# Two layers over a graph on one core: fewer completion signals from the matrix engine, and more edges counted instead of gathered

## The chip, the core and the metric

The kernel runs on one core of a Trainium2 chip. The metric is the device time of one launch in microseconds. Three runs of the kernel before took 3515.92, 3524.63 and 3525.21 us; the median is 3524.63 us.

The engines have separate instruction queues and signal each other with semaphores. PE multiplies matrices, DVE and ACT work on vectors, POOL issues indirect DMAs (it gathers rows of a table by a list of indices), and SP issues plain DMAs. "PEld" in the profile is PE's loading of the operand that stays in the array. Products land in PSUM[...].

## What is computed

There are 12500 nodes with 32 features, and 200000 edges sorted by their target `dst`. Two residual layers follow each other:

```python
h = relu(layernorm(x))
# layer 0
h  = h * rsqrt(max(out_degree, 1))[:, None]
x  = x + (segment_sum(h[src], dst) * rsqrt(max(in_degree, 1))[:, None]) @ W + b
h = relu(layernorm(x))
# layer 1, for each edge
msg = concat([h[dst], h[src] - h[dst]])
m   = relu(relu(relu(msg @ W1 + b1) @ W2 + b2) @ W3 + b3) @ W4 + b4
x   = x + segment_sum(m, dst) / max(count(dst), 1)[:, None]
```

## The kernel before

Edges are handled in tiles of 128 and chunks of four tiles (`TPC` = 4, 512 edges, 391 chunks). The order on each engine is the order in which the program is written out: the code is traced under a manual schedule, and generators (`scale_rows`, `multiply`, `count_edges`, `update_nodes`) are advanced by hand so that their stages interleave.

**Degrees.** For each batch of `HG` groups of `HT` = 4 tiles DVE makes two one-hot tiles (`hi`, `lo`, line 325) from the upper and lower part of `src`, and PE adds their products (line 342) into one table of counts. Three buffers of each exist. Meanwhile POOL gathers the raw rows of the first `EARLY` = 64 chunks (`rows_early`). After the degrees, the normalised features are split into three bf16 terms and written to the table `tab_hn`.

**Layer 0.** The chunks go three ways:
- The first 64 chunks were gathered before the degrees were known. `scale_rows` looks their scale up by one-hot products (`look`, line 664), scales the rows, and sums them by target with `sum_rows` (line 628) into `ps_early`; every fourth chunk the sum is added to an accumulator.
- Chunks 64 to `DIR` - 1 are gathered, four indirect DMAs a chunk (`gather_chunk`, line 211), and summed by `sum_rows` into `ps_late`, two steps later (`LAG`). Eight buffers `rows` lie between POOL and PE.
- The `ND` tiles from chunk `DIR` on are not gathered, but counted: for a tile, three products of one-hots (line 766) give a table of how often each of 98 x 128 sources is used by each of 13 targets, ACT copies each of the three ranges of the table out of PSUM (line 767), and `multiply` multiplies the counts of eight tiles with the whole table of features, kept in SBUF, by 98 products (line 721). The result is turned and put in its place by `L730` and `L740`.

One loop drives all this: step `m` gathers chunk `m`, prepares a one-hot for chunk `m + 2`, advances the counting by its share of `stages`, advances `scale_rows` and one stage of one `update_nodes`, and sums chunk `m - 2`. A group of 512 nodes whose sums are complete is queued for `update_nodes`, which has six stages (lines 474 to 514) and ends by writing the two tables `tab_i` and `tab_j` of the second layer. Updates run one after another.

**Layer 1.** 196 pairs of chunks pass through a pipeline. At step `m`, POOL gathers the eight tiles of pair `m` from `tab_j` (`gj`, six buffers), and PE runs the fourth product of pair `m - 5` (sum by target, line 918), the third of `m - 4` (line 900), the second of `m - 3` (line 888) and the first of `m - 1` (transposes of the gathered rows, line 870, and the products with the target rows, line 874). ACT applies the first two relus (lines 878 and 891), DVE the third (line 903).

Of the kernel before, what the change touches and what calls it, by code (L numbers as in the profile page):

```python
# [8 lines left out]
F32 = mybir.dt.float32  # L9
BF16 = mybir.dt.bfloat16  # L10
# [6 lines left out]
P = 128  # L17
# [3 lines left out]
HID = 64  # L21
# [28 lines left out]
NQ = -(-NBLK // J)  # L50


HG, HT = 2, 4
AHEAD_HG = 3


EARLY = 4 * GRP * J
# [4 lines left out]

DIR = 300
ND = NTR - DIR * TPC
TD = 8
GD = TD // TPC
# [16 lines left out]
def gnn_kernel(  # L85
# [497 lines left out]
    def halves(m):  # L583
        return [k for k in range(2) if 2 * m + k < NCH]
# [4 lines left out]
    with tc.tile_pool(name="e0", bufs=8) as sp, tc.tile_pool(name="nu", bufs=1) as np_, tc.tile_pool(  # L589
# [26 lines left out]
                count_h[:, None, :width, :].to_broadcast([P, n, width, 2]), op=OP.is_equal)  # L616
            return hot

        def hot_ahead(g, name="hot", bufs=AHEAD + 4):
            hots[g] = one_hots(sp, rel_h[:, g * TPC : (g + 1) * TPC], W, name, bufs)  # L620

        def sum_rows(g):
            k, i = divmod(g, GRP)
            if i == 0:
                group_ps[k] = pp.tile([D3, SPAN], F32, name="ps_late" if g >= EARLY else "ps_early")
            ps, rows, hot = group_ps[k], rows_of.pop(g), hots.pop(g)
            for t in range(TPC):
                nc.tensor.matmul(  # L628
                    ps[:, STEP * i : STEP * i + W], rows[:, t, :], hot[:, t // 2, :, t % 2], start=(i == 0 and t == 0),
                    stop=(i == GRP - 1 and t == TPC - 1), skip_group_check=True)  # L630
# [8 lines left out]
        def scale_rows(g):  # L639

            row = sp.tile([PART, CHUNK], F16, name="srow", bufs=2)
            nc.sync.dma_start(row, bass.AP(
                tensor=hi_row.tensor, offset=hi_row.offset + g * CHUNK, ap=[[0, PART], [1, CHUNK]]))
            yield
            turned = sp.tile([PART, CHUNK], BF16, name="sturned", bufs=2)
            nc.vector.tensor_scalar(turned, row, part_s[:PART], None, op0=OP.is_equal)
            h = rows_early[:, g, :, :D]
            if g < RAW:
                m = sp.tile([P, TPC], F32, name="raw_m", bufs=2)
                nc.vector.tensor_reduce(m, h, AX.X, OP.add)  # L650
                nc.vector.tensor_scalar(m, m, 1.0 / D, None, op0=OP.mult)
                nc.vector.tensor_sub(h, h, m[:, :, None].to_broadcast([P, TPC, D]))
                square = sp.tile([P, TPC, D], F32, name="raw_sq", bufs=2)
                nc.scalar.activation(square, h, AF.Square)
            yield
            if g < RAW:
                nc.vector.tensor_reduce(m, square, AX.X, OP.add)
                nc.vector.tensor_scalar(m, m, 1.0 / D, EPS, op0=OP.mult, op1=OP.add)
                sd = sp.tile([P, TPC], F32, name="raw_sd", bufs=2)
                nc.scalar.activation(sd, m, AF.Sqrt)  # L660
            ps = pp.tile([P, TPC, P], F32, name="look")
            for t in range(TPC):
                for k in range(3):
                    nc.tensor.matmul(
                        ps[:, t, :], turned[:, t * P : (t + 1) * P], rn3[:, k], start=(k == 0), stop=(k == 2))
            yield
            w = factors[g % 2]
            for t in range(TPC):
                c = g * TPC + t
                mask = sp.tile([P, P], F32, name="mask", bufs=2)  # L670
                nc.vector.scalar_tensor_tensor(
                    mask, lanes_s, lo_early[:, c : c + 1], ps[:, t, :], op0=OP.is_equal, op1=OP.mult,
                    accum_out=w[:, t : t + 1])
            scaled = ps[:, 0, :].rearrange("p (t c) -> p t c", t=TPC)
            if g < RAW:
                nc.vector.reciprocal(m, sd)
                nc.vector.tensor_tensor(w, w, m, op=OP.mult)

            nc.vector.scalar_tensor_tensor(
                scaled, h, 0.0, w[:, :, None].to_broadcast([P, TPC, D]), op0=OP.max, op1=OP.mult)  # L680
            rows = rows_of[g] = sp.tile([P, TPC, D3], BF16, name="rows_scaled", bufs=2)
            nc.scalar.activation(rows[:, :, 3 * D :], rows_early[:, g, :, D:], AF.Copy)
            for k in range(3):
                part = rows[:, :, k * D : (k + 1) * D]
                nc.scalar.activation(part, scaled, AF.Copy)
                if k < 2:
                    nc.vector.tensor_sub(scaled, scaled, part)
            hot_ahead(g, "hot_e", 2)
            yield
            sum_rows(g)  # L690
            yield
            add_rows(g)


        table = dp.tile([P, PART, P], BF16, name="table")
# [6 lines left out]
        def onehots_of(i):  # L702

            if i % TPC == 0:
                c = DIR * TPC + i
                los[i // TPC] = one_hots(dp, hl[:, 1, c : c + TPC], P, "lo", 3)
            onehots[i // 2] = oh = dp.tile([P, 3, KW, 2], BF16, name="oh", bufs=3)
            for k, (a, b) in enumerate(THIRDS):
                n = (b - a) * WD
                nc.vector.tensor_tensor(  # L710
                    oh[:, k, :n], keys[:, k, None, i : i + 2].to_broadcast([P, n, 2]), count_h[:, :n], op=OP.is_equal)

        def multiply(g):

            c, tiles = counts.pop(g), min(TD, ND - g * TD)

            ps = pp.tile([P, P + STEP], F32, name="st2")
            n = 3 * TD - 6
            for s in range(n):
# [27 lines left out]
        def count_edges():  # L747


            before = iter(())  # L750
            onehots_of(0)
            for i in range(ND):
                g, t = divmod(i, TD)
                if t == 0:
                    for _ in before:
                        yield
                    if g > 0:
                        before = multiply(g - 1)
                    counts[g] = dp.tile([P, TD, PART, WD], BF16, name="count", bufs=2)
                if i % 2 == 0 and i + 2 < ND:  # L760
                    onehots_of(i + 2)
                oh, lo = onehots[i // 2], los[i // TPC]
                for k, (a, b) in enumerate(THIRDS):
                    n = (b - a) * WD
                    ps = pp.tile([P, KW], F32, name="count_ps", bufs=2)
                    nc.tensor.matmul(ps[:, :n], lo[:, i % TPC // 2, :, i % 2], oh[:, k, :n, i % 2], start=True, stop=True)  # L766
                    nc.scalar.activation(  # L767
                        counts[g][:, t, a:b, :], ps[:, :n].rearrange("p (h d) -> p h d", d=WD), AF.Copy)
                    next(before, None)
                    yield  # L770
            for _ in before:
                yield
            for _ in multiply(NDG - 1):
                yield

        counting = count_edges()
        LAG = 2
        steps, stages = DIR - EARLY - 6, 3 * (ND + 2 * TD)
        for m in range(EARLY, DIR + LAG + 1):
            if m < DIR:  # L780
                rows_of[m] = sp.tile([P, TPC, D3], BF16, name="rows")
# [25 lines left out]
    with tc.manual_schedule(), tc.tile_pool(name="prep", bufs=3) as prep, tc.tile_pool(name="e1", bufs=3) as ep, tc.tile_pool(name="fn", bufs=2) as fp, tc.tile_pool(  # L807
# [2 lines left out]


        sums = Sums(fp, P, "acc1")
        group_ps, running = {}, []

        def finish_nodes(q):
# [50 lines left out]
        def first(m):  # L866
            v = live[m]
            p1 = pp1.tile([P, TPC, P], F32, name="p1")
            for t in range(TPC):
                nc.tensor.matmul(  # L870
                    p1[:, t, :], v["gj"][:, t].rearrange("p k c -> p (k c)"), ident, is_transpose=True,
                    start=(t == 0), stop=False, skip_group_check=True)
# [8 lines left out]
        def second(m):  # L881
            v = live[m]
            v["hot"] = [hot_of(ep, 2 * m + k, f"hot{k}", 4) for k in halves(m)]
            v["h2"] = []
            p2s = [pp2.tile([P, CHUNK], F32, name=f"p2{k}") for k in halves(m)]
            for k in halves(m):
                s = slice(k * HID, (k + 1) * HID)
                nc.tensor.matmul(p2s[k], w2s[s, :], v["h1"][s, :], start=True, stop=True)  # L888
            for k in halves(m):
                h2 = ep.tile([P, CHUNK], F32, name=f"h2{k}")  # L890
                nc.scalar.activation(h2, p2s[k], AF.Relu, bias=b2s)  # L891
                v["h2"].append(h2)

        def third(m):
            v = live[m]
            n = len(halves(m)) * TPC
            p3 = pp2.tile([P, 2 * TPC, HID], F32, name="p3")
            for k in halves(m):
                for t in range(TPC):
                    nc.tensor.matmul(  # L900
                        p3[:, k * TPC + t, :], v["h2"][k][:, t * P : (t + 1) * P], w3s, start=True, stop=True)
            h3 = ep.tile([P, 2 * TPC, HID], F32, name="h3")
            nc.vector.tensor_tensor(  # L903
                h3[:, :n], p3[:, :n], b3n[:, None, :].to_broadcast([P, n, HID]), op=OP.max)
# [2 lines left out]
        def fourth(m):  # L907
# [1 line left out]
            k4, i = divmod(m, GRP // 2)  # L909
            last = m == NPAIR - 1 or i == GRP // 2 - 1  # L910
            if i == 0:
                group_ps[k4] = pp2.tile([P, SPAN - STEP], F32, name="ps1", bufs=2)
            ps = group_ps[k4]
            o = 2 * STEP * i
            for t in range(TPC):
# [192 lines left out]
```

## Time and profile before

| | us |
|---|---|
| median of three runs | 3524.63 |
| the profiled execution | 4293.07 |
| its span, from first to last instruction | 4291.3 |
| first `rows_early` gather from the table starts | 52.24 |
| last degree one-hot (L325) ends | 418.3 |
| first `rows` gather starts | 476.89 |
| last `rows` gather starts | 1929.45 |
| first `gj` gather starts | 1954.60 |
| last `gj` gather starts | 4263.69 |

The profiled execution is 22% longer than the median of the timed runs, so times read from it need a check against the timed runs. The busy times by stage, with columns of stretch, its length, the busy time of PE, PEld, DVE, ACT and POOL with their instructions, the granted clock of PE, and the share and rate of DMA:

```profile
60.00:418.00 358.00, 167.92 (x1497) 125.16 (x1495) 210.63 (x428) 0.00 (x0) 205.70 (x219) 1.00 0.10 12
480.00:1925.00 1445.00, 912.03 (x8145) 681.77 (x8145) 706.89 (x2261) 665.96 (x1697) 884.06 (x938) 0.76 0.18 28
1955.00:4263.00 2308.00, 1684.26 (x8634) 1005.43 (x8636) 663.86 (x1314) 411.02 (x806) 1472.75 (x1562) 0.70 0.23 51
```

No row is full in any stage. In the groups, "busy" is the union of the instructions' times, the next number the mean of one in ns, and what stands behind the bar is the engine's idle time just before them with those that ended it. A line of the timeline has start, duration, engine, line, operation and operands, and in brackets the idle time before it and what ended it.

### The profile page before, as it was taken

Reading aid. Unit: us, or ns where it says so; the run is one execution under the profiler, and the core shown is the slowest. Engines: PE = TensorE matmul, PEld = TensorE weight load, DVE = VectorE, ACT = ScalarE, POOL = GpSimd, SP = SyncE. Lnnn points to the kernel's source line nnn. Section 1 sums busy time; section 2 is a strip of 40 time slices with the busy share of each in tenths; the row PEclk is TensorE's granted clock in tenths of the full one; section 3 lists DMA queues with packets and bytes.
Section 4 is the critical chain, followed back from the end, with each engine's and each line's share of the span. In section 5 each row is a group of like instructions: output and inputs, shape, how many; then the busy total and the mean of one; then the engine's idle time right before and its main releaser. Section 6 shows DMA issues by size and latency. Waiting matters only on the chain.

```text
span 4291.3 us, 50527 instructions
## 1 busy us (share of the span) xinstructions
PE 2813.3 (66%) x18596; PEld 1846.0 (43%) x18596; DVE 1680.5 (39%) x4199; ACT 1108.3 (26%) x2568; POOL 2616.7 (61%) x2783
## 2 busy tenths in 40 slices
PE   2444256666666666652677777777777776777778
PEld 1333144455544455431444444444444444444445
DVE  6656455554555555321223232233222222222234
ACT  0000244444444445420111111111111111111112
POOL 6554356656666656565666666666666666666663
PEclk9999977877778777765677776776767677667778
DMA  3100311111111111121122222222222222222221
GB/s 78 11 11 10 63 21 22 29 25 28 27 28 28 27 27 23 21 40 37 46 51 51 51 51 53 52 51 51 52 54 49 54 51 51 51 51 52 51 52 36
DMA packets 238472, 173.61 MB, mean 40 GB/s; under 512 B 157810, under 2 KB 186706, under 8 KB 238218
## 3 DMA queue, kind: packets, MB, share of 16 engines
q0 software_dynamic: 88416, 79.14, 11.5%
q1 hardware_dynamic: 131306, 85.26, 7.5%
q10 hardware_dynamic: 18496, 5.89, 0.9%
q8 instruction: 151, 2.47, 0.2%
q14 instruction: 103, 0.84, 0.1%
HBM read 157.16 MB, written 12.92 MB: 40 GB/s over the span
## 4 chain that ended last, share of the span: by engine, by line
PE 31%; another core or an unknown queue 11%; issue 10%; POOL 6%; DVE 4%; ACT 1%; DMA 0%; ACTq 0%; DVEq 0%; POOLq 0%
PE p L900 8%; POOL gj L211 6%; PE p L888 6%; PE p L874 5%; PE ps L918 4%; PE p L870 3%; PE st L721 1%; PE count_ps L766 1%; DVE hot L575 1%; DVE h L903 1%; DVE turned L854 1%; ACT count L767 1%; PE kept L831 1%; PE ps_late L628 0%
## 5 line engine op out<-in xcount | busy, mean ns | idle before, releaser
L211 POOL DMA_INDIRECT gj<-tab_j,src_j x1563 | 1474.5, 943 | 859.8 <-issue 443.6
L211 POOL DMA_INDIRECT rows<-tab_hn,src_j x944 | 890.7, 944 | 624.8 <-issue 234.2
L766 PE MATMUL count_ps<-oh,lo 128*128 128x429 bf16 x1089 | 468.4, 442 | 384.4 <-issue 182.6
L767 ACT ACTIVATE count<-count_ps 128x429 bf16<-128x429 f32 x1089 | 547.1, 524 | 577.3 <-remote 184.4
L903 DVE TENSOR_TENSOR h<-p,b3n 128x512 f32<-128x512 f32 x196 | 135.2, 690 | 1250.9 <-remote 607.6
L900 PE MATMUL p<-w3s,h 128*128 128x64 f32 x3128 | 504.8, 315 | 129.2 <-issue 118.5
L891 ACT ACTIVATE h<-p,b2s 128x512 f32<-128x512 f32 x391 | 253.3, 685 | 1253.3 <-remote 519.8
L721 PEld LDWEIGHTS <-table 128*128 128x128 bf16 x4508 | 378.0, 115 | 429.2 <-issue 386.4
L900 PEld LDWEIGHTS p<-w3s,h 128*128 128x128 f32 x3128 | 464.4, 228 | 173.8 <-issue 155.8
L721 PE MATMUL st<-count,table 128*128 128x104 bf16 (+1 forms) x4508 | 446.0, 243 | 9.0 <-issue 9.0
L888 PE MATMUL p<-h,w2s 64*128 64x512 f32 x782 | 388.2, 844 | 69.8 <-issue 68.5
L874 PE MATMUL p<-turned,ai 128*64 128x512 f32 x782 | 367.3, 842 | 52.4 <-issue 51.7
L918 PE MATMUL ps<-hot,h 128*64 128x128 f32 x3126 | 283.9, 332 | 174.3 <-DVE h L903 126.4
L918 PEld LDWEIGHTS ps<-hot,h 128*64 128x64 f32 x3126 | 240.1, 172 | 345.9 <-DVE h L903 219.5
L870 PE MATMUL p<-ident,gj 128*128 128x128 f32 x784 | 206.5, 362 | 168.1 <-issue 132.9
L342 PE MATMUL deg_ps<-hi,lo 128*128 128x98 bf16 x1563 | 175.6, 271 | 196.3 <-DVE lo L325 116.2
L211 POOL DMA_INDIRECT rows_early<-tab_h,src_j x224 | 211.3, 943 | 151.6 <-DVE src_j L334 84.8
L710 DVE TENSOR_TENSOR oh<-keys,kept 128x858 bf16<-128x858 f16 x546 | 291.5, 589 | 12.7 <-PE count_ps L766 6.7
L870 PEld LDWEIGHTS p<-ident,gj 128*128 128x128 f32 x784 | 114.8, 174 | 398.2 <-issue 353.2
L854 DVE TENSOR_TENSOR turned<-row,kept 128x512 f32<-128x512 f16 x391 | 249.4, 679 | 26.0 <-PE p L874 13.7
L575 DVE TENSOR_TENSOR hot<-rel_h,kept 128x512 f32<-128x512 f16 x391 | 249.1, 678 | 0.0
L342 PEld LDWEIGHTS <-lo 128*128 128x128 bf16 x1563 | 131.0, 126 | 240.9 <-DVE lo L325 143.0
(197 smaller groups left out, 2333.8 us busy)
## 6 DMA issues: line engine op xcount, KB each, us to landing
row<-rel_row SPq DMA_DIRECT2D x195, 256.0 KB
gj<-tab_j,src_j POOLq DMA_INDIRECT x1563
rows<-tab_hn,src_j POOLq DMA_INDIRECT x944
ai<-tab_i SPq DMA_DIRECT2D x195, 64.0 KB
srow<-hi_row SPq DMA_DIRECT2D x64, 98.0 KB
rows_early<-tab_h,src_j POOLq DMA_INDIRECT x224
tab_j<-nu_aij SPq DMA_DIRECT2D x24, 128.0 KB
tab_i<-nu_aij SPq DMA_DIRECT2D x24, 128.0 KB
```

The source lines that it names most:

```text
L211: nc.gpsimd.indirect_dma_start(out=tile_ap, out_offset=None, in_=table, in_offset=bass.IndirectOffsetOnAxis(ap=col, axis=0))
L342: nc.tensor.matmul(deg_ps, lo[:, g, :, i], hi[:, g, :, i], start=(t == 0), stop=(t == NTR - 1))
L575: nc.vector.tensor_tensor(hot, rel_h[:, g * TPC : (g + 1) * TPC][:, :, None].to_broadcast([P, TPC, W]), lanes_f[:, None, :W].to_broadcast( ...
L721: nc.tensor.matmul(ps[:, : tiles * WD], table[:, h, :], c[:, :tiles, h, :], start=(h == 0), stop=(h == PART - 1))
L766: nc.tensor.matmul(ps[:, :n], lo[:, i % TPC // 2, :, i % 2], oh[:, k, :n, i % 2], start=True, stop=True)
L767: nc.scalar.activation(counts[g][:, t, a:b, :], ps[:, :n].rearrange("p (h d) -> p h d", d=WD), AF.Copy)
L854: nc.vector.tensor_tensor(turned, v["row"][:, k], part_f.to_broadcast([P, CHUNK]), op=OP.is_equal)
L870: nc.tensor.matmul(p1[:, t, :], v["gj"][:, t].rearrange("p k c -> p (k c)"), ident, is_transpose=True, start=(t == 0), stop=False, skip_gr ...
L874: nc.tensor.matmul(p1[k * HID : (k + 1) * HID].rearrange("p t e -> p (t e)"), v["ai"][:, k], v["turned"][k], start=False, stop=True, skip_ ...
L888: nc.tensor.matmul(p2s[k], w2s[s, :], v["h1"][s, :], start=True, stop=True)
L900: nc.tensor.matmul(p3[:, k * TPC + t, :], v["h2"][k][:, t * P : (t + 1) * P], w3s, start=True, stop=True)
L918: nc.tensor.matmul(ps[k * HID : (k + 1) * HID, o : o + W], v["h3"][:, k * TPC + t, :], v["hot"][k][:, t, :], start=(i == 0 and t == 0), st ...
```

## The change

- **Degrees**: a batch has four groups of four tiles instead of two (`HG`), and the early gathers run two batches ahead instead of three.
- **Split of layer 0**: `DIR` goes from 300 to 268, so 816 tiles are gathered instead of 944, and 491 counted instead of 363. `stages` counts four stages a tile instead of three.
- **Counting**: the one-hots of a pair of tiles are made by one DVE operation instead of three. The first two ranges of the counts land in a tile of two banks (`count_two`) and leave by one ACT operation; the third has a bank of its own (`count_third`). Each has one buffer, where `count_ps` had two. The three stages of `multiply` are advanced before a tile's products, not between them.
- **Early chunks** are summed one by one in the bank of `look` and added at once; `ps_early` is gone.
- **Layer 1**: a product of one column, which reads an element of each of the eight gathered tiles, stands ahead of the transposes, so that one place waits for a pair's rows. The two second products share a tile of two banks and one relu of 1024 columns. `p3` has two buffers instead of one, and the two sums `ps1` share one bank (`both`).

```diff
-HG, HT = 2, 4
-AHEAD_HG = 3
+HG, HT = 4, 4
+AHEAD_HG = 2
...
-DIR = 300
+DIR = 268
...
             yield
-            sum_rows(g)
+
+            total = ps[:D3, 1]
+            for t in range(TPC):
+                nc.tensor.matmul(
+                    total, rows[:, t, :], hot[:, t // 2, :, t % 2], start=(t == 0), stop=(t == TPC - 1))
             yield
-            add_rows(g)
+            sums.add(slice(0, D3), STEP * g, total)
+            added([g])
...
-            for k, (a, b) in enumerate(THIRDS):
-                n = (b - a) * WD
-                nc.vector.tensor_tensor(
-                    oh[:, k, :n], keys[:, k, None, i : i + 2].to_broadcast([P, n, 2]), count_h[:, :n], op=OP.is_equal)
+            nc.vector.tensor_tensor(
+                oh, keys[:, :, i : i + 2][:, :, None, :].to_broadcast([P, 3, KW, 2]),
+                count_h[:, None, :, :].to_broadcast([P, 3, KW, 2]), op=OP.is_equal)
...
-                for k, (a, b) in enumerate(THIRDS):
-                    n = (b - a) * WD
-                    ps = pp.tile([P, KW], F32, name="count_ps", bufs=2)
-                    nc.tensor.matmul(ps[:, :n], lo[:, i % TPC // 2, :, i % 2], oh[:, k, :n, i % 2], start=True, stop=True)
-                    nc.scalar.activation(
-                        counts[g][:, t, a:b, :], ps[:, :n].rearrange("p (h d) -> p h d", d=WD), AF.Copy)
+                for _ in range(3):
                     next(before, None)
                     yield
+
+                for ranges, name in ((THIRDS[:2], "two"), (THIRDS[2:], "third")):
+                    k0, a, b = THIRDS.index(ranges[0]), ranges[0][0], ranges[-1][1]
+                    ps = pp.tile([P, len(ranges), 512], F32, name=f"count_{name}")
+                    w = (b - a) // len(ranges) * WD
+                    for k in range(len(ranges)):
+                        nc.tensor.matmul(
+                            ps[:, k, :w], lo[:, i % TPC // 2, :, i % 2], oh[:, k0 + k, :w, i % 2], start=True, stop=True)
+                    nc.scalar.activation(
+                        counts[g][:, t, a:b, :].rearrange("p (k h) d -> p k (h d)", k=len(ranges)), ps[:, :, :w], AF.Copy)
+                yield
...
-        steps, stages = DIR - EARLY - 6, 3 * (ND + 2 * TD)
+        steps, stages = DIR - EARLY - 6, 4 * (ND + 2 * TD)
...
+        both = pp2.tile([P, 2, SPAN - STEP], F32, name="ps1")
...
+            nc.tensor.matmul(
+                p1[:1, 0, : 2 * TPC], ident[:, :1], v["gj"][:, :, :, 0].rearrange("p t k -> p (t k)"), start=True, stop=True,
+                skip_group_check=True)
...
-            p2s = [pp2.tile([P, CHUNK], F32, name=f"p2{k}") for k in halves(m)]
+            n = len(halves(m))
+            p2 = pp2.tile([P, 2, CHUNK], F32, name="p2")
             for k in halves(m):
                 s = slice(k * HID, (k + 1) * HID)
-                nc.tensor.matmul(p2s[k], w2s[s, :], v["h1"][s, :], start=True, stop=True)
-            for k in halves(m):
-                h2 = ep.tile([P, CHUNK], F32, name=f"h2{k}")
-                nc.scalar.activation(h2, p2s[k], AF.Relu, bias=b2s)
-                v["h2"].append(h2)
+                nc.tensor.matmul(p2[:, k], w2s[s, :], v["h1"][s, :], start=True, stop=True)
+            h2 = v["h2"] = ep.tile([P, 2, CHUNK], F32, name="h2")
+            nc.scalar.activation(h2[:, :n], p2[:, :n], AF.Relu, bias=b2s)
...
-            p3 = pp2.tile([P, 2 * TPC, HID], F32, name="p3")
+            p3 = pp2.tile([P, 2 * TPC, HID], F32, name="p3", bufs=2)
...
-                group_ps[k4] = pp2.tile([P, SPAN - STEP], F32, name="ps1", bufs=2)
+                group_ps[k4] = both[:, k4 % 2]
```

More of the change, by code (lines that the diff above doesn't have):

```diff
@@ L617, in one_hots, with hot_ahead @@
             return hot
-        def hot_ahead(g, name="hot", bufs=AHEAD + 4):
-            hots[g] = one_hots(sp, rel_h[:, g * TPC : (g + 1) * TPC], W, name, bufs)
+        def hot_ahead(g):
+            hots[g] = one_hots(sp, rel_h[:, g * TPC : (g + 1) * TPC], W, "hot", AHEAD + 4)
         def sum_rows(g):
@@ L624, in sum_rows @@
             if i == 0:
-                group_ps[k] = pp.tile([D3, SPAN], F32, name="ps_late" if g >= EARLY else "ps_early")
+                group_ps[k] = pp.tile([D3, SPAN], F32, name="ps_late")
             ps, rows, hot = group_ps[k], rows_of.pop(g), hots.pop(g)
@@ L680, in scale_rows @@
                 scaled, h, 0.0, w[:, :, None].to_broadcast([P, TPC, D]), op0=OP.max, op1=OP.mult)
-            rows = rows_of[g] = sp.tile([P, TPC, D3], BF16, name="rows_scaled", bufs=2)
+            rows = sp.tile([P, TPC, D3], BF16, name="rows_scaled", bufs=2)
             nc.scalar.activation(rows[:, :, 3 * D :], rows_early[:, g, :, D:], AF.Copy)
@@ L687, in scale_rows @@
                     nc.vector.tensor_sub(scaled, scaled, part)
-            hot_ahead(g, "hot_e", 2)
+            hot = one_hots(sp, rel_h[:, g * TPC : (g + 1) * TPC], W, "hot_e", 2)
             yield
-            sum_rows(g)
+            total = ps[:D3, 1]
+            for t in range(TPC):
+                nc.tensor.matmul(
+                    total, rows[:, t, :], hot[:, t // 2, :, t % 2], start=(t == 0), stop=(t == TPC - 1))
             yield
-            add_rows(g)
+            sums.add(slice(0, D3), STEP * g, total)
+            added([g])
         table = dp.tile([P, PART, P], BF16, name="table")
@@ L883, in second @@
             v["hot"] = [hot_of(ep, 2 * m + k, f"hot{k}", 4) for k in halves(m)]
-            v["h2"] = []
-            p2s = [pp2.tile([P, CHUNK], F32, name=f"p2{k}") for k in halves(m)]
+            n = len(halves(m))
+            p2 = pp2.tile([P, 2, CHUNK], F32, name="p2")
             for k in halves(m):
                 s = slice(k * HID, (k + 1) * HID)
-                nc.tensor.matmul(p2s[k], w2s[s, :], v["h1"][s, :], start=True, stop=True)
-            for k in halves(m):
-                h2 = ep.tile([P, CHUNK], F32, name=f"h2{k}")
-                nc.scalar.activation(h2, p2s[k], AF.Relu, bias=b2s)
-                v["h2"].append(h2)
+                nc.tensor.matmul(p2[:, k], w2s[s, :], v["h1"][s, :], start=True, stop=True)
+            h2 = v["h2"] = ep.tile([P, 2, CHUNK], F32, name="h2")
+            nc.scalar.activation(h2[:, :n], p2[:, :n], AF.Relu, bias=b2s)
         def third(m):
@@ L900, in third @@
                     nc.tensor.matmul(
-                        p3[:, k * TPC + t, :], v["h2"][k][:, t * P : (t + 1) * P], w3s, start=True, stop=True)
+                        p3[:, k * TPC + t, :], v["h2"][:, k, t * P : (t + 1) * P], w3s, start=True, stop=True)
             h3 = ep.tile([P, 2 * TPC, HID], F32, name="h3")
```

## The prediction, made before the changed kernel ran

> **What bounds the kernel now.** I read the page's totals first, then its groups for POOL, then the waits of POOL, then the timeline at the seams between stages. No engine is full on the page: PE 66%, POOL 61%. POOL's gathers (line 211) are the only work that runs through all stages:
>
> ```profile
> PE 2813.3 (66%) x18596; PEld 1846.0 (43%) x18596; DVE 1680.5 (39%) x4199; ACT 1108.3 (26%) x2568; POOL 2616.7 (61%) x2783
> ...
> L211 POOL DMA_INDIRECT gj<-tab_j,src_j x1563 | 1474.5, 943 | 859.8 <-issue 443.6
> L211 POOL DMA_INDIRECT rows<-tab_hn,src_j x944 | 890.7, 944 | 624.8 <-issue 234.2
> ...
> L211 POOL DMA_INDIRECT rows_early<-tab_h,src_j x224 | 211.3, 943 | 151.6 <-DVE src_j L334 84.8
> ```
>
> A gather is busy 0.943 us and is followed by 0.30 us that belong to it; the timeline of POOL shows the pitch, and the seam from the first layer to the second:
>
> ```profile
> 1928.20 0.94 POOL L211 DMA_INDIRECT rows<-tab_hn,src_j  x1 [0.30 <-issue]
> 1929.45 0.94 POOL L211 DMA_INDIRECT rows<-tab_hn,src_j  x1 [0.30 <-issue]
> 1954.60 0.94 POOL L211 DMA_INDIRECT gj<-tab_j,src_j  x1 [24.20 <-DMA row<-rel_row]
> 1955.84 0.94 POOL L211 DMA_INDIRECT gj<-tab_j,src_j  x1 [0.30 <-issue]
> ```
>
> The pitch is 1.249 us (1929.45 - 1928.20, and the same almost everywhere). The rest of POOL's idle time, about 810 us (1647 us in the four gather groups less 2763 x 0.303), sits in some 360 holes of 1.3 to 6 us. The timeline shows what they are: PE has finished its products, nobody sees it, and PE itself goes on at 0.7 us or more an instruction:
>
> ```profile
> 3030.27 2.00 PE L900 MATMUL p<-w3s,h 128*128 128x64 f32 x16
> ...
> 3035.13 0.59 PE L888 MATMUL p<-h,w2s 64*128 64x512 f32 x1 [1.51 <-issue]
> ...
> 3037.93 0.37 PE L870 MATMUL p<-ident,gj 128*128 128x128 f32 x1 [1.15 <-issue]
> ...
> 3041.41 0.94 POOL L211 DMA_INDIRECT gj<-tab_j,src_j  x1 [3.58 <-PE p L870]
> 3041.60 0.69 DVE L903 TENSOR_TENSOR h<-p,b3n 128x512 f32<-128x512 f32 x1
> ```
>
> L900 ended at 3032.27, and L903, which reads it, began at 3041.60. Are these holes in the timed runs? The profiled execution took 4293.1 us (span 4291.3 and 1.8 around it), the timed runs 3524.6. Without holes POOL alone gives: first gather of the table at 52.2, 2730 pitches of 1.249 = 3409.8, the seam's extra 23.9, and 27.6 from the last gather's start (4263.7) to the end, plus 1.8: 3515 us. The timed runs are 3515.9 to 3525.2. So I take the timed kernel to be a bare chain of gathers with one seam, and the holes to belong to the profiled execution. The median stands 9 us above that sum; I anchor on the median and use differences.
>
> Is the first stage (degrees, to 418) inside this chain? DVE's pair of L325 repeats every 1.07 us where nothing holds it (200.55, 201.62 on the timeline), so 196 batches take 210 us from 48.8, with 5 for `src_j`, to 264; from L325's end to the first `rows` gather the profile needs 58.6 us (418.3 to 476.9), which gives 322. The 224 early gathers end at 52.2 + 280 = 332. POOL is the later by 10 us.
>
> **What the Trainium skill says.** "TensorE: Matmul & The Clock Gate", The cost: per-tile semaphore tail, prices an increment at 26.3 ns. The built program has 4195 PE updates before and 2641 after, so at most 1554 x 26 ns = 41 us of PE's own time, an estimate; no row of this trace isolates it. The same page, Part 1, lets the clock be half or full by recent activity: the windows agree (0.50 at the seam, 0.70 to 0.76 mean in the two layers), so a busier PE should get the full clock. "PSUM — Partial Sum Buffer", PSUM bank collisions, wants readers and writers of a bank apart; that is why one bank for two sums (`both`) means waiting. "Perfetto Trace Analysis", DMA Instruction — SWDGE, says the row of a gather is descriptor generation, not transport; the constant 943 ns agrees.
>
> **The change part by part.**
>
> *Gathers.* DIR 300 -> 268 makes 32 chunks of 4 gathers into 128 counted tiles. POOL: 128 x 1.249 = -159.9 us, on the path.
>
> *Counting in the time that is left.* A step of the loop is four gathers, 5.0 us. Counting now must put 491 tiles into 268 - 64 - 6 = 198 steps, 2.48 a step; before 363 in 230, 1.58. PE's prices at full clock, from this piece of the timeline:
>
> ```profile
> 1214.47 0.35 PE L766 MATMUL count_ps<-oh,lo 128*128 128x429 bf16 x1
> ...
> 1214.66 0.47 PE L721 MATMUL st<-count,table 128*128 128x104 bf16 x6
> ...
> 1214.97 0.83 PE L664 MATMUL look<-rn,sturned 98*128 98x128 bf16 x12
> ...
> 1215.66 0.39 PE L628 MATMUL ps_late<-hot,rows 128*97 128x128 bf16 x4
> ...
> 1215.89 0.35 PE L766 MATMUL count_ps<-oh,lo 128*128 128x429 bf16 x1
> ```
>
> From start to start: L766 0.19, L721 0.052, L664 0.058, four L628 0.23. A tile is 3 x 0.19 + 12.25 x 0.052 = 1.21; a step 2.48 x 1.21 = 3.0, plus rows 0.23, a third of look and its sum 0.30, placing (L730, L740; 1.2 per eight tiles) 0.37, node updates (3.3 us each, 25 in 204 steps) 0.4: 4.3 of 5.0 us. ACT: two evacuations instead of three. A form of 429 took 528 ns, of 416 516, 512 columns 596 and 128 columns 279, so 0.83 ns a column; 858 in one is 0.88 (estimate). Consecutive ones overlap by 0.11 (three in 1.50 us at 1217.83), so 0.77 + 0.40 = 1.17 a tile, 2.9 a step, some 3.6 with the rest. DVE: one `oh` of 2574 instead of 858 + 858 + 832; three took 1.60, the merged one about 1.4; with one-hots, masks and sums some 3.8 a step. All three stay under 5.0, and eight `rows` buffers let PE trail by about six steps. The new bank pair (`count_two`, one buffer) closes a loop: evacuation 0.88, two products and their end 0.5, about 0.1 of signalling: 1.5 a tile, 3.7 a step. I cost all this at nothing; POOL's gathers hide it. If the cover goes, each 0.1 us a tile over 2.0 costs 49 us.
>
> *The seam.* This I did not expect from the diff. Node updates go one after another, one stage a step. In the built order two are evacuated (L511) after the last `rows` gather before the change, five after it; one of these five is at its end, as one was just before the gather earlier, so two more full updates stand with POOL idle, since the first `gj` gather reads the whole of `tab_j`. The loop is 32 steps shorter, and the last early chunks, the last counted tiles and the last gathered ones now finish together. One update lasts from 1939.8 (L474) to 1950.7 (`tab_j` issued), 10.8 us, a chain through PE, DVE and ACT. +2 x 10.8 = +21.7. Bounds: 0 if they are done while rows arrive, 33 if three count.
>
> *Degrees.* 98 double batches save about 0.07 us of fixed cost twice per pair: 14 us of DVE, but POOL ends later there: 0 (to -9, the unexplained rest). The keys of 128 more tiles add about 1 us, covered alike.
>
> *Sums of early chunks in `look`.* The bank is held until DVE has added; the next look comes three steps after the previous, and its add is issued in the same step just ahead: 0, within PE's slack.
>
> *Second layer.* A pair has 8 x 1.249 = 10.0 us of POOL. PE's work on a pair at a mostly full clock, from L918 at 3042.34 to L918 at 3049.21, is 6.9. The added tiny product waits for all eight rows at once; behind it stand four transposes, two products and relu, and `gj` has six buffers. One relu of 1024 columns, one wait on `both`, two `p3`: all in the 3 us of slack. POOL's 1563 gathers stay: 0. Tail +1 (joined relu, last rows waited for together), -1 (fewer updates): 0.
>
> Sum: -159.9 + 21.7 = -138. In the profile's own terms 3515 - 138 = 3377; on the median, 3386.
>
> **Rivals.**
> *Counting becomes the bound, mildly* (0.17). For: 4.3 of 5.0 us on an in-order queue that also waits. At 2.2 us a tile 491 tiles take 1080 us where the gathers need 984 (198 steps): about +90, 3476. Against: PE's stretches without holes run near the price above.
> *The holes are in the timed runs* (0.06). For: they hit what waits on PE, and the change cuts those updates by 37%. Scaled by 3525/4291, the 810 us are 665, 37% of that is 246, and 128 gathers at 1.03 are 131: 3148. Against: the sum of 3515 leaves no room for them.
> *Counting by turns, slower* (0.12). With `count_two` and `count_third` single, PE's products and ACT's evacuations could alternate instead of overlapping: 1.17 + 1.21 + 0.48 of other PE work = 2.86 us a tile, 491 tiles 1404 us, against 984: +420 on 3386, 3806. It decides from 2.3 us a tile (984 + 138 = 1122 over 491). For: before, `count_ps` had two buffers, and PE waited 154.9 us there for ACT. Against: st2's products stand between two tiles in PE's order and run during the evacuation.
> *No effect* (0.02): the seam and a slowed count eat exactly the gain.
>
> **How the numbers follow.** POOL bound as computed: 0.63, own range 3360 to 3410. With the mild rival the range goes to 3480; low 3360 covers no cost at the seam. Left out: the turns, the holes. What a measurement can tell is 0.3%, 10.6 us. Faster is 0.63 + 0.17 + 0.06, and a sliver of the slow rival, 0.87; same 0.03; slower 0.10.
>
> **What would show it.** Right: `gj` pitch 1.249 unchanged; between first and last `rows` gather 816 gathers with holes no more frequent; five L511 after the last of them and a seam of some 45 us; evacuations of 858 near 0.88. Wrong: `rows` gathers waiting on PE in places where PE is not crawling but waiting on ACT or DVE; a timed gain under 100 or over 165 us.

## The result, and the profile after

The changed kernel took 3635.39 us (median of four runs, 3634.06 to 3637.26) where the kernel before took 3524.29: ratio 1.0321, interval 1.0308 to 1.0333. It is 111 us slower; the prediction was 3386.

The kernel before takes about 3515 to 3525 us where the change was measured and on one chip of the experiments, and about 4309 us on three other chips that the experiments fell on, so every comparison below is between runs side by side on one chip, unless it says otherwise. Below, a pitch is the time from the start of one gather to the next, and the gaps of POOL that the prediction calls holes are called so here too.

The profiled execution of the changed kernel (span 3635.5 us) is like its timed runs. From its page, the totals and five groups, in the form shown for the kernel before:

```profile
PE 2615.8 (72%) x20860; PEld 1844.5 (51%) x20860; DVE 1749.5 (48%) x3784; ACT 1186.7 (33%) x2348; POOL 2506.5 (69%) x2655
...
L211 POOL DMA_INDIRECT gj<-tab_j,src_j x1563 | 1478.3, 946 | 515.9 <-issue 421.7
L211 POOL DMA_INDIRECT rows<-tab_hn,src_j x816 | 772.2, 946 | 502.4 <-PE ps_late L628 280.3
L777 ACT ACTIVATE count<-count_two 128x858 bf16<-128x858 f32 x491 | 434.5, 885 | 347.8 <-PE count_two L775 319.3
...
L881 PE MATMUL p<-gj,ident 128*1 128x8 f32 x392 | 39.1, 174 | 509.4 <-DMA gj<-tab_j,src_j 509.4
L713 DVE TENSOR_TENSOR oh<-keys,kept 128x2574 bf16<-128x2574 f16 x246 | 365.4, 1487 | 71.0 <-PE count_third L775 70.9
```

In layer 1 the 0.30 us behind each gather is all that POOL waits, and PE waits for the gathers: layer 1 is a bare chain of gathers. In layer 0 it is the other way round: POOL waits 280 us for PE, and these waits are for the products of rows (L628), which free the `rows` buffers.

The timeline of POOL at the seam:

```profile
1611.86 0.95 POOL L211 DMA_INDIRECT rows<-tab_hn,src_j  x1 [0.30 <-issue]
1613.11 0.95 POOL L211 DMA_INDIRECT rows<-tab_hn,src_j  x1 [0.30 <-issue]
1653.66 0.95 POOL L211 DMA_INDIRECT gj<-tab_j,src_j  x1 [39.61 <-DMA row<-rel_row]
```

Between the first `rows` gather (339.73) and the last lie 1273.4 us; 815 pitches of 1.249 would be 1018. The difference, 255 us, is the whole surprise: 3386 + 255, and 5 less for a seam of 40.6 instead of 45, is 3636. The evacuations of the third range end from 328.7 to 1578.9, so a counted tile takes 2.55 us; 2.0 would have kept pace with the gathers.

The windows of layer 0 and layer 1 (columns as before):

```profile
345.00:1580.00 1235.00, 929.17 (x9758) 701.93 (x9758) 757.32 (x1950) 756.58 (x1633) 742.37 (x785) 0.88 0.16 26
1660.00:3600.00 1940.00, 1445.43 (x9013) 951.20 (x9014) 668.40 (x1313) 382.25 (x614) 1467.09 (x1552) 0.80 0.27 60
```

In layer 0 nothing is full: PE 75%, DVE and ACT 61%, POOL 60%. The timeline shows how the counting still falls behind:

```profile
900.72 1.00 PE L724 MATMUL st<-count,table 128*128 128x104 bf16 x16 [0.77 <-DVE nu_c L478]
...
901.55 0.55 PE L775 MATMUL count_two<-oh,lo 128*128 128x429 bf16 x2
...
901.94 0.35 PE L775 MATMUL count_third<-oh,lo 128*128 128x416 bf16 x1
...
902.20 0.89 ACT L777 ACTIVATE count<-count_two 128x858 bf16<-128x858 f32 x1 [1.12 <-PE count_two L775]
902.98 0.51 ACT L777 ACTIVATE count<-count_third 128x416 bf16<-128x416 f32 x1
903.38 0.20 ACT L550 ACTIVATE acc_e<-look 97x32 f32<-97x32 f32 x1
...
903.63 0.83 PE L664 MATMUL look<-rn,sturned 98*128 98x128 bf16 x12 [1.34 <-ACT acc_e L550]
...
904.30 0.40 PE L628 MATMUL ps_late<-hot,rows 128*97 128x128 bf16 x4
...
904.97 0.95 POOL L211 DMA_INDIRECT rows<-tab_hn,src_j  x1 [2.44 <-PE ps_late L628]
```

ACT stands 1.12 us waiting for PE's `count_two`. Behind these two evacuations in ACT's queue is a copy of 0.20 us, the first part of an early chunk's sum out of `look`. PE's next product into `look` waits for it, 1.34 us; the rows product stands behind that, and POOL behind the rows product. So PE waits for ACT, which had waited for PE.

### The profile page after: what moved, and what is told of

Same layout as the page of the kernel before. It is cut to its first block, busy times and chain, and to the rows that moved or that the text cites. A ratio compares the mean times of both kernels' runs of the same rounds, so it can differ in the third digit from the quotient of the medians.

```text
span 3635.5 us, 54239 instructions
## 1 busy us (share of the span) xinstructions
PE 2615.8 (72%) x20860; PEld 1844.5 (51%) x20860; DVE 1749.5 (48%) x3784; ACT 1186.7 (33%) x2348; POOL 2506.5 (69%) x2655
## 5 line engine op out<-in xcount | busy, mean ns | idle before, releaser
L211 POOL DMA_INDIRECT rows<-tab_hn,src_j x816 | 772.2, 946 | 502.4 <-PE ps_late L628 280.3
L777 ACT ACTIVATE count<-count_two 128x858 bf16<-128x858 f32 x491 | 434.5, 885 | 347.8 <-PE count_two L775 319.3
L913 PE MATMUL p<-w3s,h 128*128 128x64 f32 x3128 | 444.2, 302 | 0.2 <-ACT h L905 0.2
L913 PEld LDWEIGHTS p<-w3s,h 128*128 128x128 f32 x3128 | 416.3, 214 | 47.5 <-issue 38.3
L905 ACT ACTIVATE h<-p,b2s 128x1024 f32<-128x1024 f32 x196 | 218.0, 1112 | 661.8 <-PE p L903 661.8
L713 DVE TENSOR_TENSOR oh<-keys,kept 128x2574 bf16<-128x2574 f16 x246 | 365.4, 1487 | 71.0 <-PE count_third L775 70.9
L893 ACT ACTIVATE h<-p 128x512 f32<-128x512 f32 x196 | 117.1, 597 | 793.7 <-PE p L889 793.7
L881 PEld LDWEIGHTS p<-gj,ident 128*1 128x1 f32 x392 | 21.7, 80 | 681.9 <-issue 663.7
L775 PE MATMUL count_two<-oh,lo 128*128 128x429 bf16 x982 | 303.0, 393 | 78.6 <-ACT count L777 68.0
L552 DVE TENSOR_TENSOR acc<-acc,ps 64x64 f32<-64x64 f32 (+1 forms) x198 | 44.7, 226 | 526.1 <-PE ps L931 493.4
L777 ACT ACTIVATE count<-count_third 128x416 bf16<-128x416 f32 x491 | 251.3, 512 | 0.0
```

The costliest lines, as they stand in the source:

```text
L211: nc.gpsimd.indirect_dma_start(out=tile_ap, out_offset=None, in_=table, in_offset=bass.IndirectOffsetOnAxis(ap=col, axis=0))
L713: nc.vector.tensor_tensor(oh, keys[:, :, i : i + 2][:, :, None, :].to_broadcast([P, 3, KW, 2]), count_h[:, None, :, :].to_broadcast([P, 3, ...
L775: nc.tensor.matmul(ps[:, k, :w], lo[:, i % TPC // 2, :, i % 2], oh[:, k0 + k, :w, i % 2], start=True, stop=True)
L777: nc.scalar.activation(counts[g][:, t, a:b, :].rearrange("p (k h) d -> p k (h d)", k=len(ranges)), ps[:, :, :w], AF.Copy)
L905: nc.scalar.activation(h2[:, :n], p2[:, :n], AF.Relu, bias=b2s)
L913: nc.tensor.matmul(p3[:, k * TPC + t, :], v["h2"][:, k, t * P : (t + 1) * P], w3s, start=True, stop=True)
```

## The experiments

Theories that return below: P, PE itself is the chain in layer 0, so each of its waits costs its time; T, PE and ACT take turns over the single `count_two`; B, the holes go away when PE updates fewer semaphores. When T and P had both failed in part, the parts of the change were set side by side. `ps_late`, `look`, `st` (`st2` in the code) and `count_two` are buffers of PSUM (banks) that PE fills and ACT or DVE empties.

**The four first (before: 4307.8).** They fell on a chip where the kernel before has holes too, so of their expectations, which were made for 3515 us, only the signs can be read. The changed kernel with `DIR` 300:

```diff
-DIR = 268
+DIR = 300
```

> The changed kernel with DIR back at 300 (363 counted tiles). Two theories of the 254 us that POOL waited for PE in layer 0 of the changed kernel. Amount: a counted tile costs about 2.55 us there (last evacuation less first, 1250 us over 490), whatever limits it, and 491 of them no longer fit beside the gathers; then 363 x 2.55 = 926 us fit under 944 x 1.25 = 1180 us of gathers, the rows gathers hardly wait for PE, and the time is 3500 to 3540 us. Form: the new way of counting or summing is itself slow and takes gathers with it; then rows gathers still wait, and the time is over 3560 us.

4335.67 us, ratio 1.0074 (1.0050 to 1.0097). With the old number of tiles the other edits together still lose 28 us; PE waits 48.4 us at `look` for ACT's copy (29 times, 500 to 1850).

The kernel before with `DIR` 268:

```diff
-DIR = 300
+DIR = 268
```

> The kernel before with DIR at 268 (491 counted tiles, old counting). Amount: the old counting does not fit either, 3580 to 3700 us. Form: the old counting with two buffers keeps up, 3380 to 3420 us as the prediction computed for the changed kernel.

4351.69 us, 1.0099 (1.0078 to 1.0120). More tiles alone already lose, 44 us.

The kernel before with the layer 1 edits alone (one product ahead of the transposes, joined relu, two `p3`, `both`):

> The kernel before with only the edits of the second layer (one wait for a pair's rows, joined second products, one bank for two sums). Both theories: POOL bounds that layer, 3515 to 3530 us, no change. If the fewer updates of PE matter in timed runs, faster by over 10 us. Its profile also tells whether the holes of the profile of before (PE's end seen late) come from the updates that these edits remove: then they are gone in the second layer and stay in layer 0.

4298.35 us, 0.9980 (0.9968 to 0.9991): 0.2%, which no stage of its profile shows. The `gj` stage keeps its holes, 362 us in all where before has 360, so they don't come from the updates of PE that these edits remove.

The changed kernel with the old counting loop (`stages` set back to three a tile):

```diff
-                for ranges, name in ((THIRDS[:2], "two"), (THIRDS[2:], "third")):
...
+                for k, (a, b) in enumerate(THIRDS):
+                    n = (b - a) * WD
+                    ps = pp.tile([P, KW], F32, name="count_ps", bufs=2)
...
```

> The changed kernel with the old three evacuations a tile (count_ps, two buffers) between the products, all else as changed. Form (the two-bank tile without a second buffer is the brake): 3380 to 3450 us. Amount: 3600 us or more; ACT has 147 more evacuations than in the changed kernel's two a tile, so it may even be slower than 3635.

4412.77 us, 1.0254 (1.0231 to 1.0277). The changed kernel itself was not yet measured beside it.

**Where to loosen the ring (before: 3514.6).**

> The changed kernel once more, as it is, to have it beside its variants and beside the kernel before on one chip. The kernel before took 3524 us where the change was measured and 4308 us where the first four kernels ran; there the holes of 1.3 to 6 us were in the timed runs. Theory A (the holes belong to the chip or the execution, whatever the kernel): where the kernel before takes about 3524, this takes 3635, ratio 1.032; where it takes about 4308, this has holes too and takes 4308 + 100 to 150, ratio 1.02 to 1.035. Theory B (the holes go when TensorE updates fewer semaphores): it takes about 3635 where the kernel before takes 4308, ratio 0.84.

3630.45 us, 1.0333 (1.0316 to 1.0350): the result again. Theory B of the holes could not be tested here, since the kernel before had none.

One stage more ahead of the transposition of `some`:

```diff
             nc.scalar.activation(some[:, : tiles * WD], ps[:D3, : tiles * WD], AF.Copy)
             yield
+            yield
```

> One stage more between the evacuation of a group's second product (`some`, ScalarE) and its transposition by TensorE, where TensorE waits 76 us in 53 places. Theory P (in the first layer TensorE itself is the chain: 929 us busy and 306 us of waits in 1235, so a wait taken from it is time won): 40 to 75 us less than the unchanged kernel of this call. Theory T (TensorE and ScalarE take turns over the pair of banks `count_two`; other waits of TensorE only shift): within 15 us of the unchanged kernel, and the wait of `count_two` for ScalarE grows by what goes here.

3628.41 us, 2 less. PE's wait there hardly moved (72.4 to 69.4 us): in the order of the program the added stage comes before the tile's products, so that no counting of PE stands between the two. So it says little on either theory; a stronger form follows below.

First sums of layer 0 copied by DVE:

```diff
-                    nc.scalar.activation(a, ps[:, :n], AF.Copy)
+                    if self.rows == D3:
+                        nc.vector.tensor_copy(a, ps[:, :n])
+                    else:
+                        nc.scalar.activation(a, ps[:, :n], AF.Copy)
```

> In the first layer the first sum of a range is copied by VectorE in place of ScalarE (line 550), so that `ps_late` and `look` are released by VectorE alone; TensorE waits 52 + 47.5 us for these copies. Theory P: 50 to 100 us less than the unchanged kernel. Theory T: ScalarE has 80 copies of 0.3 to 0.6 us less to do between its evacuations, so 15 to 40 us less, and TensorE's wait at `count_two` grows. A third theory (VectorE is the late one): slower, up to 30 us.

3553.90 us, 1.0113 (1.0096 to 1.0130): 77 less. P named this size, T half of it or less. PE's waits between 345 and 1500 (us in all, times, longest), first in the unchanged kernel:

```profile
PE st L733 <- ACT some L730: 72.4, 50, 2.7
PE count_two L775 <- ACT count L777: 51.0, 58, 3.9
...
PE ps_late L628 <- ACT acc_t L550: 48.8, 26, 3.6
PE look L664 <- ACT acc_e L550: 46.8, 51, 1.4
```

and with the copies on DVE (lines three further down):

```profile
PE st L736 <- ACT some L733: 76.3, 53, 2.7
PE count_two L778 <- ACT count L780: 60.4, 64, 4.1
...
PE ps_late L631 <- DVE acc_t L551: 43.9, 20, 3.5
...
PE look L667 <- DVE acc_e L551: 3.2, 5, 0.7
```

The wait at `look` is gone, the one at `ps_late` nearly stays. The wait was 47 us and the kernel won 77; in which waits the other 30 us stood isn't shown. DVE's busy time in the same window rose from 715 to 781 us of 1155, and the kernel still gained: DVE had room.

Half of the second products left out:

```diff
                 for h in range(PART * s // n, PART * (s + 1) // n):
+                    if h % 2 and h != PART - 1:
+                        continue
```

> Leaves out every second head of the second products (line 724: 50 of 98 in place of 98 a group), so the sums of the counted tiles lack them; evacuations, one-hots and the order stay. It takes 48 x 62 products of TensorE away, 0.05 to 0.07 us each: 150 to 210 us of TensorE's work in the first layer. Theory P: the first layer comes near the pace of the gathers, 130 to 200 us less than the unchanged kernel. Theory T (products fill the time of the evacuations, which sets the pace): less than 60 us less.

This kernel leaves those products out of its sums. 3619.62 us, 11 less, against P's 130 to 200; T's "less than 60" holds. PE's busy time in the window fell only from 869 to 802 us. The window has 2694 products less, some 140 us by the prediction's price of 0.052, and the granted clock fell from 0.89 to 0.81: (869 - 140) x 0.89/0.81 = 801, so by this estimate the lower clock took the rest back. Even of the 67 us only 11 were won. PE's waits for ACT in the window rose from 270 to 332 us in all, so most of what was taken away came back as waiting, above all here (51.0 in the unchanged kernel):

```profile
PE count_two L777 <- ACT count L779: 107.5, 154, 4.4
```

So the amount of PE's work alone isn't the bound. Since the remaining products ran at the lower mean clock, the run doesn't say what shorter products would do.

**The parts, set side by side.** Three kernels ran first on a chip with holes on which the changed kernel itself wasn't measured (before: 4309.3):

> The kernel before with 491 counted tiles (DIR 268) and nothing else of the change, again, on a chip where the gathers have no holes. Theory N (the number of tiles is the cause: 491 in 198 steps is more than the three engines can pass, whatever the buffers): as slow as the changed kernel or slower, 3600 to 3680 us (2.4 to 2.6 us a tile). Theory E (the edits to the counting loop are the cause: single pair of banks, sums in `look`): under 3500 us, near 3400.

4346.73 us, 1.0100 (1.0060 to 1.0140). This chip had holes, so the figures of the expectation don't apply; the sign is N's.

> The changed kernel with the old counting loop (three ranges a tile, each with its own product and evacuation, two buffers `count_ps`), the sums of early chunks still in `look`. Theory T (turns over the single pair `count_two` set the pace): 50 us or more less than the changed kernel (3630). Theory C (what counts is how often ScalarE is asked for an evacuation that TensorE waits for, and its time: 1.5 us a tile in three against 1.4 in two): slower than the changed kernel, 3640 to 3720.

4407.47 us, 1.0240 (1.0201 to 1.0279).

First copies by DVE for the early sums alone (the condition that changes against the edit of all first sums):

```diff
-                    if self.rows == D3:
+                    if self.rows == D3 and q < QE:
```

> The changed kernel, where only the first copy of an early chunk's sum (`acc_e` from `look`, line 550, 64 copies of 0.20 us) goes from ScalarE to VectorE; all first sums on VectorE gave 77 us. If the bank `look`, held until ScalarE comes to the copy, was the cost of the sums in `look`: 45 to 75 us less than 3630. If it was the copies from `ps_late` or ScalarE's load in general: under 25 us less.

4331.79 us, 1.0057 (1.0037 to 1.0078).

Then the same three beside the changed kernel (before: 4309.5):

> The changed kernel as it is, beside its parts in one call. On a chip where the kernel before takes about 3515 us: 3630, as twice before. Where it takes about 4309: with holes, 4370 to 4420 (4332 was measured there with the first copies of early sums on VectorE, 4407 with the old counting loop); 3630 there would say that the changed kernel has no holes on any chip.

> The kernel before with 491 counted tiles and nothing else of the change. Where the kernel before takes about 3515 us: theory N (491 tiles are more than the three engines pass in the time of the gathers, with the old loop too): 3560 to 3680. Theory E (the edits to the loop are the cause): 3390 to 3450. Where it takes about 4309: 4347 again, and its place beside the changed kernel tells what all other edits do together.

> The changed kernel with the old counting loop (two buffers of one range, three evacuations a tile). Theory T (turns over the single pair set the pace): 40 us or more less than the changed kernel of this call. Theory C (evacuating two ranges at once is a help, and the rest is slow): 15 to 90 us more.

> The changed kernel, where only the first copy of an early chunk's sum goes from ScalarE to VectorE. If the hold of `look` for ScalarE is the cost of summing in `look`: 45 to 75 us less than the changed kernel of this call; if the other first copies gave the 77 us that all of them gave: under 25 less.

| kernel | us | ratio, interval | first to last `rows` gather | seam |
|---|---|---|---|---|
| before (stage and seam from the profile shown above, an execution of 4293) | 4309.5 | | 1452.6 | 25.1 |
| before, `DIR` 268 | 4345.8 | 1.0082, 1.0052 to 1.0111 | 1470.5 | 45.9 |
| changed, old counting loop | 4405.2 | 1.0223, 1.0204 to 1.0243 | 1528.6 | 45.9 |
| changed | 4410.5 | 1.0230, 1.0211 to 1.0250 | 1540.1 | 47.0 |
| changed, early copies by DVE | 4333.9 | 1.0068, 1.0046 to 1.0091 | 1451.2 | 46.9 |

Read from the top. More counted tiles alone: +36; in the stage, 128 gathers less (-160), and +178 for a count that is late (+181 and +195 in the profiles of the two earlier runs of this kernel), and +21 at the seam. All other edits: +65. Of these the pairing comes to nothing: the old loop with two buffers is 5 us faster, within the intervals, where theory T asked for 40 or more. The old loop has a buffer more and an evacuation more a tile, so the run shows their sum, not each. And moving the first copies of the early sums (61 in the trace, of 0.20 us) to another queue takes 77 us away, more than the other edits had added: with `look` freed they come out 12 us under more tiles alone, within the intervals, the merged one-hots and the products put ahead included. Theory B of the holes falls too: the changed kernel has them where the kernel before has them.

**Is each wait of PE worth its time?** On top of the early copies by DVE (before: 3513.2):

```diff
             nc.scalar.activation(some[:, : tiles * WD], ps[:D3, : tiles * WD], AF.Copy)
             yield
+            yield
+            yield
```

> As the kernel with the early sums' first copies on VectorE (4332 and 4334 us where the kernel before takes 4309; all first copies there gave 3554 where it takes 3515), and the transposition of `some` three stages after its evacuation in place of one, so that a tile's counting stands between them on TensorE; one stage more, without such work between, had moved 2 us. TensorE waits 77 us there in 54 places. Theory W (each wait that stands in TensorE's queue is worth its time, as the wait at `look` was): 40 to 75 us less. Theory X (only `look` was worth it, since its release went round by ScalarE behind evacuations that wait for TensorE; this wait shifts to the next evacuation): within 15 us, or slower by up to 30, since TensorE's work no longer fills the evacuation of that tile.

3618.80 us, 1.0295 (1.0278 to 1.0312). The kernel without the two stages wasn't measured beside it; the nearest, all first copies by DVE, had taken 3553.9 where before took 3514.6. PE's waits (345 to 1500):

```profile
PE count_two L780 <- ACT count L782: 83.3, 73, 4.7
PE st L727 <- ACT acc_d L553: 65.2, 52, 2.8
PE st L748 <- ACT some_t L740: 60.6, 44, 5.7
...
PE st L738 <- ACT some L733: 1.4, 1, 1.4
```

The wait for `some` went from 76 us to 1, and two new ones of 65 and 61 us came: the bank `st2` is now held longer, so the next group's first product waits for it, and `some_t` is copied behind evacuations. That is theory X, and worse than the 30 us that it allowed: the wait moved on and grew. The edit also makes the counting of eight tiles one stage longer, 33 in place of 32.

**Fewer tiles with the copies on DVE.**

```diff
-DIR = 268
+DIR = 284
```

> All first sums on VectorE as before, and 427 counted tiles in place of 491 (DIR 284). The counting took 2.35 us a tile with 491; 427 tiles in 214 steps of 5.0 us leave 2.5. If a tile costs the same here, the gathers are the bound again: 3515 - 80 + 20 = 3455 us, ratio 0.98. If the cost of a tile grows as the work is packed otherwise: 3480 to 3520.

4262.00 us where before took 4309.3: 0.9899 (0.9860 to 0.9938).

> All first sums on VectorE with 427 counted tiles (DIR 284) again. Where the kernel before takes about 4309: 4262 again, ratio 0.99. Where it takes about 3515: 3455 with the gathers as the bound (3515 - 64 x 1.249 + 20 at the seam), ratio 0.983; 3480 to 3520 if the counting still holds them.

3483.57 us where before took 3513.2: 0.9907 (0.9890 to 0.9923). It beats the kernel before by 0.9%, and the changed kernel (3630.45 on the same chip). The 28 us above the 3455 are a late count: `rows` gathers still stand 40 us over their pitch, and the seam is 31.4 us, less than assumed.

## Why the prediction was wrong, by its own steps

*The bare chain of gathers*: right as a sum. In the profile after, the early gathers end at 339.4 (forecast 332, and POOL later than DVE, as said: L325 ends at 252.7), the `gj` pitch is 1.251 throughout (1953.7 us for 1562), and 28.2 us follow the last gather's start. The 810 us of holes were 724: 62 of the idle time stand between the early gathers and the first `rows` gather, and 24 at the seam. Wrong in whose the holes are: they belong neither to the profiling nor to the kernel, since timed runs have them on three of the experiments' chips and not on the fourth.

*Gathers, -159.9*: held. *Degrees, layer 1, tail, 0*: held. *The seam, +21.7*: +20.8 in the pair that differs in `DIR` alone; 40.6 us after against the 45 forecast. Four L511 follow the last `rows` gather, not five; two more than before, as the sum had it.

*Counting, 0*: this is the step that failed, in its sentence "All three stay under 5.0" and in what it drew from it, "I cost all this at nothing". The loads were nearly right. An evacuation of 858 took 0.885 (forecast 0.88), the merged `oh` 1.49 (1.4). Over some 490 tiles the window gives ACT 1.54 and DVE 1.55 us a tile, times 2.48 tiles a step 3.8 each (3.6 and 3.8), and PE 1.90, so 4.7 (4.3; the granted clock was 0.88, where the prediction expected the full clock). All are under 5.0, yet a step took 2.55 x 2.48 = 6.3 us. PE waited 306 of the 1235 us, 1.5 us a step, 289 of them for ACT. Loads by engine bound a stage from below only. What each of three in-order queues waits for the next, when they hand the same banks on, comes on top; that this makes up all of the difference is argued from the waits, not shown. The sentence after it, on lost cover, was right in size: 0.55 us over 2.0 at 49 us a tenth is 270, measured 255.

*Sums of early chunks in `look`, "0, within PE's slack"*: wrong by 77 us of the 255, as the runs with these copies on DVE show. The step asked when the add is issued, not which queue it stands in. Before, the copies of four early chunks were made together from a bank of their own; now `look` is handed back 61 times through ACT, behind evacuations that wait for PE. It costs 1.3 us each for a copy of 0.20.

The rest, some 178 us, most likely comes with the number of tiles: `DIR` 268 alone loses 178 to 195 us in the stage, with the old loop. This was measured on chips with holes only; on the chip without, that kernel wasn't run, and there the `rows` gathers of the changed kernel with the copies on DVE still stand 177 us over their pitch.

*The rivals.* "Counting by turns" named the sign and the point from which it decides (2.3 us a tile), but not the mechanism: it blamed the single `count_two`, and the old loop with two buffers came out the same. Its size, 420 us, was too large, and "mildly the bound", 90, too small. The rival with holes in the timed runs fails for the runs that it spoke of; it would be right for three other chips, but not in what it drew from it: fewer updates of PE take no holes away.

Open: why the count takes 2.39 us a tile even with `look` set free (all first copies on DVE). Less PE work moved little and one wait moved elsewhere; no run isolates the remaining 178 us, and which of PE's waits for ACT sets the pace stays open. More buffers for the pair weren't tried beside the freed `look`.

## What to carry to other kernels

Adding up each engine's load shows only how fast a stage can be at best. Where in-order engines pass buffers to one another, count what is handed on as well: here 2.48 tiles a step failed at a PE load of 4.7 us in 5.0, and still at 4.3 with half of the second products gone; 2.0 tiles (427 in 214 steps) with the copies on DVE nearly held, at 3.9. For every buffer, ask in whose queue the operation that frees it stands and what that queue waits for: here a copy of 0.2 us, late in its queue, cost over a microsecond. When work is moved from a bound engine to others, try a smaller dose: with the copies on DVE, and both against the kernel before, 64 tiles moved gained 30 us where 128 lost 39.

## What the runs showed of the hardware

The same kernel took 3512 to 3520 us on one chip of the experiments and 4294 to 4327 on three. In all 13 profiles with the long times, POOL's `gj` gathers have holes of 358 to 376 us in all, whatever is changed: 360 in the kernel before, 362 with the layer 1 edits, 359 with `DIR` 300, 362 in the changed kernel. In the profiles from the chip with the short times and in the profile after, they have at most 0.2. So neither the number of PE's updates nor the work of layer 0 makes these holes; what does is open.

With half of the second products gone, PE's granted clock in the window fell from 0.89 to 0.81, so work of some 140 us (an estimate from the prediction's price) lowered PE's busy time by 67 us only.
